# Local attention and whitening on one core: when a new image's terms are moved, four wider shuffles, copied weights straight from DRAM, and VectorE's share of the last image

## The chip, the cores and the metric

The kernel runs on one core of one Trainium2 chip. The metric is the device time of one execution in microseconds (us). The engines named below are TensorE (PE in the profile, with PEld for its weight loads), VectorE (DVE), ScalarE (ACT), GpSimd (POOL) and SyncE (SP). In this kernel SP and POOL mostly issue DMAs, each in its own queue and in order.

## The reference, cut to what matters

```python
# layer 0: a 7x7 convolution with dilation 2 (256 -> 128), a 1x1 one (128 -> 49),
# a softmax over the 49 taps, and a sum of 49 shifted inputs with those weights
k = lax.conv_general_dilated(x, w1, (1, 1), [(6, 6), (6, 6)], rhs_dilation=(2, 2), dimension_numbers=DN) + b1[None, :, None, None]
k = lax.conv_general_dilated(k, w2, (1, 1), [(0, 0), (0, 0)], dimension_numbers=DN) + b2[None, :, None, None]
attn = jax.nn.softmax(k, axis=1)
xp = jnp.pad(x, ((0, 0), (0, 0), (6, 6), (6, 6)))
shifts = jnp.stack([xp[:, :, 2*u:2*u + H, 2*v:2*v + W] for u in range(7) for v in range(7)], axis=1)
x = jnp.einsum('bkchw,bkhw->bchw', shifts, attn)
# layer 1: iterative whitening of each of 4 groups of 64 channels over all pixels
Sigma = EPS * I + jnp.einsum('gdm,gem->gde', xc, xc) / m      # xc: x less its mean
# five Newton steps give wm, the inverse root of Sigma
X_hat = jnp.einsum('gde,gem->gdm', wm, xc)
```

x is (4, 256, 64, 64) in f32: four images of 256 channels.

## The kernel before, in words

Both convolutions are folded into one with 49 output channels, and that one is computed by a two-dimensional fast convolution: rows and columns of the input are combined at seven evaluation points each (`EVAL`), TensorE multiplies point by point, and VectorE interpolates the results back. For an image b the row points are visited in the order `ROWS`, and for each row point the column points come in three banks, `BANKS`: (1, 2, 0), (3, 4, 6) and (5). `conv_step(k, i)` does bank i of row point k on TensorE (`conv_bank`, matmuls on L593) and then lets `prepare` get the same bank of the next row point ready: weights (`weights`, L405), row combination (`row_eval`), column combination (`col_eval`).

**Weights.** The combined weights of a row point and bank are made once, when they are first used, and written to DRAM (`gd`, store on L475); later images load them (L419). For the row points 0, 4 and 5 the row-combined weights themselves lie in DRAM (`kept`). In `weights`, f is the SBUF place that they are loaded to (load on L428): `lgx` for row point 5, the first row buffer `rb[0]` for 4 and 0. VectorE makes the combinations from f into the bank's tile wt (tag wr0, wr1 or wr2, one buffer each), and ScalarE copies those column points that need no combination (`same`, L451, L452 and L461). The first uses of 4 and 5 fall in image 1's convolution, that of 0 in image 2's first steps, which are prepared at the end of image 1's.

**Attention.** The logits of an image are transposed on TensorE into PSUM (L984, a ring of three buffers tagged tp that the other transposes share) and go through `softmax(b, pc)`, once for each parity pc of the columns: VectorE takes maxima (L990), ScalarE does 16 exponentials of 128x49 with a running sum (L998), VectorE scales (L1002 to L1011) and shifts the taps sideways by six in-place shuffles (L1017). The sums are done in quarters of an image, n = 0 to 15 (n // 4 is the image, n % 2 the parity). `move_terms(n)` copies the taps into a padded tile zt by eleven copies (L1058 on ScalarE; for the last image five of the eleven go to VectorE, L1070) and writes it to DRAM in eight DMAs of POOL's queue (L1075); `load_band(n, half)` reads it back skewed, on SP's queue (L1110, L1121). `first_half(n)` and `second_half(n)` then do the sums: `make_block` transposes pieces of the input (L1151) and copies them out of PSUM (xb, L1157, and for the middle pieces xbz, L1165), `weighted_sum` multiplies block by band (L1191), `store_y` writes the result back, `turn_y` transposes it (L1222) and copies it (yt, L1230), and `moments` adds up the Gram matrix (L1243).

**Order.** The halves and softmaxes are planned into eight gaps of each image's convolution (`plan`, `gap`); TensorE's order is the program's (`pe`). On the other engines the tile framework orders instructions by when they are ready in its model and by priority; `tc.high_priority()` raises it, and a manual dependency without a semaphore keeps an instruction behind another on one engine. What the planning does with the last half but one of an image's sums matters here: gap (b + 1, 0) holds `first_half(4b - 1)` and then `soft(b, 0)`, gap (b + 1, 1) holds `second_half(4b - 1)` and then `soft(b, 1)`, and gap (b + 1, 2) holds `first_half(4b)`, for b = 1 and 2. For b = 3 there is no convolution left around them: `second_half(10)` and `soft(3, 0)`, `first_half(11)` and `soft(3, 1)`, `second_half(11)`, `first_half(12)` and so on run one after the other. Before these, `tail` is set, and from there VectorE takes the xb copies and half of `store_y`. In `soft`, the call `bands(4 * b)` moves the new image's first terms at once.

After the sums come the Newton steps (L1441 and around) and the application of the matrices with the output (L1573, L1589).

Of the kernel before, what the change touches and what calls it, by code (L numbers as in the profile page):

```python
# [23 lines left out]
INF = 6  # L24
# [8 lines left out]
def kernel(  # L33
# [371 lines left out]
    def weights(b, br, i, mid=None):  # L405

        first = (br, i) not in made
        made.add((br, i))
        s0 = slot_of[BANKS[i][0]]
        ns = sum(len(taps(bc)) for bc in BANKS[i])
        nk = NSK * len(taps(br)) // 2
        wt = apool.tile([P, ns, NSK], F32, tag=f"wr{i}", name=f"wr_{b}_{br}_{i}")[:, :, :nk]
        w = {bc: wt[:, slot_of[bc] - s0 : slot_of[bc] - s0 + len(taps(bc))] for bc in BANKS[i]}
        if not first:
            nc.sync.dma_start(wt, gd[br][:, s0 : s0 + ns])  # L419
            return w  # L420

        if br in kept:


            f = lgx if br == 5 else rb[0].rearrange("p q r c w -> p (q r c w)")
            f = f[:, : KS * nk]
            if i == 0:
                nc.sync.dma_start(f, kept[br])  # L428
            f = f.rearrange("p (v a r k) -> p v a r k", v=KS, a=NCC, k=KT)
            g = [f[:, v] for v in range(KS)]  # L430
        else:
            g = [gbr[:, v] for v in range(KS)]
        g = [t.rearrange("p a r k -> p (a r k)") for t in g]

        e = ct.rearrange("p a b -> p (a b)") if b else store[4].rearrange("p c r w -> p (c r w)")
        e, o, e1 = (e[:, k * nk : (k + 1) * nk] for k in range(3))
        g0 = [g[KS - 1 - a] for a in range(4)]
        g1 = [g[KS - 5 - a] for a in range(3)]
        o0 = {bc: w[bc][:, 0] for bc in w}
        o1 = {bc: w[bc][:, 1] for bc in w if bc != INF}  # L440

        same = nc.scalar.copy
        if i == 0:
            add(e, g0[0], g0[2])
            add(o, g0[1], g0[3])
            add(e1, g1[0], g1[2])
            add(o0[1], e, o)
            sub(o0[2], e, o)
            add(o1[1], e1, g1[1])
            sub(o1[2], e1, g1[1])  # L450
            same(o0[0], g0[0])  # L451
            same(o1[0], g1[0])  # L452
        elif i == 1:
            madd(e, g0[2], 4.0, g0[0])
            madd(o, g0[3], 4.0, g0[1])
            madd(e1, g1[2], 4.0, g1[0])
            madd(o0[3], o, 2.0, e)
            madd(o0[4], o, -2.0, e)
            madd(o1[3], g1[1], 2.0, e1)
            madd(o1[4], g1[1], -2.0, e1)  # L460
            same(o0[INF], g0[3])  # L461
        else:
            madd(o0[5], g0[0], 2.0, g0[1])
            madd(o1[5], g1[0], 4.0, g1[2])
            madd(o0[5], o0[5], 2.0, g0[2])
            if mid is not None:
                mid()
            madd(o1[5], g1[1], 2.0, o1[5])
            madd(o0[5], o0[5], 2.0, g0[3])
            add(o1[5], o1[5], o1[5])  # L470
        for bc in BANKS[i]:
            f = SCALE[bc] * (SCALE[br] if br not in kept else 1.0)
            if f != 1.0:
                nc.scalar.mul(w[bc], w[bc], f)
        nc.sync.dma_start(gd[br][:, s0 : s0 + ns], wt)  # L475
        return w
# [497 lines left out]
    def softmax(b, pc):  # L974

        lv = logits[b].rearrange("p r w -> p (r w)")
        nm = f"{b}_{pc}"
        mx = work.tile([P, NCH, 2], F32, tag="mx", name=f"mx_{nm}")
        lt = []
        for hf in range(2):  # L980
            lt.append(tp().rearrange("p (i h k) -> p i h k", i=NI, h=2))
            for i in range(NI):
                pe(
                    nc.tensor.transpose(  # L984
                        lt[hf][:, i].rearrange("p h k -> p (h k)")[:, :K2],
                        lv[:K2, bass.ds(2 * (NI * hf + i) * P + pc, P, 2)],
                        ident[:K2, :K2],
                    )
                )
            nc.vector.tensor_reduce(  # L990
                mx[:, NI * hf : NI * (hf + 1)], lt[hf][:, :, :, :KT], AX.X, ALU.max
            )
        nc.vector.tensor_scalar(mx, mx, -1.0, None, ALU.mult)  # L993
        d = terms[b, pc] = bpool.tile([P, 2, NCH, KT], F32, tag="d", name=f"d_{nm}", bufs=2)
        s = work.tile([P, 2, NCH], F32, tag="s", name=f"s_{nm}")
        for h in range(2):
            for i in range(NCH):
                nc.scalar.activation(  # L998
                    d[:, h, i], lt[i // NI][:, i % NI, h, :KT], AF.Exp,
                    bias=mx[:, i, h : h + 1], accum_out=s[:, h, i : i + 1],  # L1000
                )
            nc.vector.reciprocal(s[:, h], s[:, h])  # L1002
            rm = work.tile([P, NCH, KS], F32, tag="rm", name=f"rm_{nm}_{h}")
            nc.vector.tensor_tensor(
                rm,
                s[:, h].unsqueeze(2).to_broadcast([P, NCH, KS]),
                cmask.unsqueeze(1).to_broadcast([P, NCH, KS]),
                ALU.mult,
            )
            dh = d[:, h].rearrange("p i (u v) -> p i u v", u=KS)  # L1010
            nc.vector.tensor_tensor(  # L1011
                dh, dh, rm.unsqueeze(2).to_broadcast([P, NCH, KS, KS]), ALU.mult
            )
        dv = d.rearrange("p h i (u v) -> p (h i u) v", u=KS)
        for v in range(KS):
            if v != R:
                last = nc.vector.stream_shuffle(  # L1017
                    dv[:, :, v], dv[:, :, v], [(c - v + R) % SW for c in range(SW)]
                )

        return last

# [5 lines left out]
    def move_terms(n, after=None):  # L1028
# [9 lines left out]
        for k, (s, j0, nj) in enumerate(MOVES):  # L1038
            u = (s + R) % CR
            m, g = divmod(j0 + u - R, CR)  # L1040
            ne = 2 if u + CR < KS else 1
            i = d[j0 * SW : (j0 + nj) * SW, :, u : u + CR * (ne - 1) + 1 : CR]
            i = bass.AP(
                tensor=i.tensor,
                offset=i[:, :, :, KS - 1].offset,
                ap=[*(list(a) for a in i.ap[:-1]), [-1, KS]],
            )
            o = zt[g * SW : (g + nj) * SW]
            e = R + KS * m + KS - 1 - u
            o = bass.AP(  # L1050
                tensor=o.tensor,
                offset=o[:, e].offset,
                ap=[list(o.ap[0]), [KS * WS, NCH], [(KS - CR) * WS, ne], [1, KS]],
            )

            with tc.high_priority() if n % 4 == 0 else nullcontext():
                if k % 2 == 0 or b < B - 1:
                    ins = nc.scalar.copy(o, i)  # L1058
                    if after is not None:

                        tc.add_manual_dep(
                            ins.ins,
                            after.ins.name,
                            mybir.DependencyInfo(
                                mybir.DependencyClass.NoSync, mybir.DependencyReason.DATA
                            ),
                            reason="move_terms",
                        )
                else:
                    nc.vector.tensor_copy(o, i)  # L1070
# [73 lines left out]
    def make_block(n, m):  # L1144
# [14 lines left out]
        if t8 in (1, 2):  # L1159
            z = ("z", 2 - t8)  # L1160
            if h == 0:
                blocks[n, z] = bpool.tile([P, C], F32, tag=f"xbz{t8}", name=f"xbz_{n}_{t8}")
            i = slice(0, 64) if t8 == 2 else slice(64, P)
            with tc.high_priority():
                nc.scalar.copy(blocks[n, z][h * 64 : (h + 1) * 64], t[i, :C])  # L1165


    PIECES = (
# [48 lines left out]
    def turn_y(n, i):  # L1217
# [9 lines left out]
            )  # L1227
        yb = ybs[n, i] = yt_buf[i % NY]
        with tc.high_priority():
            nc.scalar.copy(  # L1230
                yb.rearrange("p a g c -> p (a g) c")[:, :, :GW],
                t[:, :C].rearrange("p (e c) -> p e c", c=GW),
            )
# [76 lines left out]
    def bands(n, after=None):  # L1310

        move_terms(n, after)
        if n - 1 in half_done:
            load_band(n, 0)
        if n - 1 in done:
            load_band(n, 1)
            move_terms(n + 1, after)

    def second_half(n):
        turn_y(n, 0)  # L1320
        turn_y(n, 1)
        weighted_sum(n, 1, 0)
        weighted_sum(n, 1, 1)
        turn_y(n, 2)
# [20 lines left out]
    def soft(b, pc):  # L1345
        with tc.high_priority() if pc == 0 else nullcontext():
            last = softmax(b, pc)
        soft_done.add((b, pc))
        if pc == 0:
            bands(4 * b)  # L1350

    for b in range(B):
        hs = [
# [279 lines left out]
```

## Time and profile before

| | us |
|---|---|
| median of 3 runs | 741.79 (741.7 to 742.51) |
| the profiled execution | 740.84 |
| its span in the trace | 739.1 |
| TensorE busy in the span | 689.6 (93%) |
| VectorE busy | 581.2 (79%) |
| ScalarE busy | 355.8 (48%) |
| GpSimd busy | 133.4 (18%) |
| mean granted TensorE clock | 0.975 |

The stages as the timeline shows them, with the busy time of each engine:

| stretch (us) | what runs | PE | DVE | ACT | clock |
|---|---|---|---|---|---|
| 0 to 150 | folding of the weights, image 0's convolution | 142.4 | 127.9 | 39.5 | 1.00 |
| 150 to 306 | image 1's convolution, image 0's sums | 148.9 | 132.6 | 85.0 | 0.99 |
| 306 to 452 | image 2's, image 1's sums | 140.6 | 129.4 | 81.3 | 0.99 |
| 452 to 571 | image 3's, image 2's sums | 111.6 | 104.1 | 63.9 | 0.97 |
| 580 to 618 | last softmaxes, n = 10 to 12 | 27.8 | 23.2 | 21.9 | 0.91 |
| 618 to 669 | the other sums of image 3 | 49.9 | 17.0 | 24.2 | 1.00 |
| 669 to 683 | Newton steps | 10.1 | 8.7 | 3.5 | 0.72 |
| 683 to 739.1 | application, output | 49.9 | 32.6 | 31.0 | 0.93 |

A wait in such a profile is read from the idle time of an engine just before an instruction, with the engine and line that released it. A busy share near 100% says that the engine was the bound of that stretch only where the others waited for it.

### The profile page before, as it was taken

What the parts mean: (1) busy time and instruction counts of PE and PEld (TensorE: products, weight loads), DVE (VectorE), ACT (ScalarE), POOL (GpSimd) and SP (SyncE); (2) the same over time, 40 slices, a digit from 0 to 9 for tenths busy, and PEclk for the clock granted to TensorE, in tenths of its full rate; (3) what the DMA queues carried; (4) which work ended last, traced back from release to release, by engine and by line L of the source; (5) the groups of instructions that cost most, each with busy time, mean ns of one, the idle gap of its engine ahead of it and who ended that gap; (6) DMA issues with size and microseconds to landing.
All of it is one profiled execution on the core that took longest, in us unless ns stands there. A gap on an engine that the chain in (4) does not pass through costs nothing. (4 is left out here: it accounts for less than half of the span.)

```text
span 739.1 us, 19180 instructions
## 1 busy us (share of the span) xinstructions
PE 689.6 (93%) x7728; PEld 543.4 (74%) x7728; DVE 581.2 (79%) x1260; ACT 355.8 (48%) x1043; POOL 133.4 (18%) x194
## 2 busy tenths in 40 slices
PE   6999999999998989989999999799999878997996
PEld 1449543478997988878999989798998767895231
DVE  3799998994895899989985999799959564335575
ACT  1424320133755655756554446626546655542564
POOL 0002526664030110020221100202202023300000
PEclk9999999999999999999999999899999999997899
DMA  8923999974673671258746721353623144573587
GB/s 321 256 91 109 243 373 224 229 169 100 165 181 113 243 226 62 67 158 262 188 111 218 245 67 34 73 163 77 186 76 77 45 92 102 119 250 149 228 361 322
DMA packets 77041, 125.20 MB, mean 169 GB/s; under 512 B 36327, under 2 KB 57368, under 8 KB 75800
## 3 DMA queue, kind: packets, MB, share of 16 engines
q1 hardware_dynamic: 64664, 81.88, 34.6%
q0 software_dynamic: 12288, 42.08, 21.9%
q8 instruction: 61, 1.00, 0.6%
q14 instruction: 28, 0.23, 0.1%
HBM read 77.87 MB, written 52.36 MB: 176 GB/s over the span
## 5 line engine op out<-in xcount | busy, mean ns | idle before, releaser
L593 PE MATMUL cv<-xh,wr 128*49 128x128 f32 x4160 | 232.7, 274 | 0.0
L593 PEld LDWEIGHTS cv<-xh,wr 128*49 128x49 f32 x4160 | 227.7, 125 | 3.2 <-issue 1.3
L1075 POOL DMA_DIRECT2D sd<-zt x128 | 67.5, 533 | 324.1 <-ACT zt L1058 290.2
L1191 PE MATMUL y<-band,xb 128*128 128x209 f32 x512 | 115.2, 353 | 3.3 <-DMA band<-sd 2.7
L1191 PEld LDWEIGHTS y<-band,xb 128*128 128x128 f32 x512 | 89.5, 198 | 5.1 <-DMA band<-sd 3.2
L604 ACT COPY pv<-cv 113x486 f32<-113x486 f32 (+2 forms) x60 | 26.0, 433 | 96.2 <-PE cv L593 95.9
L1222 PE MATMUL tp<-ident,slot 128*128 128x128 f32 x256 | 52.9, 304 | 17.9 <-ACT yt L1230 11.0
L1222 PEld LDWEIGHTS tp<-ident,slot 128*128 128x128 f32 x256 | 41.0, 205 | 26.7 <-ACT yt L1230 12.8
L1230 ACT COPY yt<-tp 128x256 f32<-128x256 f32 x128 | 45.3, 376 | 31.5 <-PE tp L1222 30.0
L1058 ACT COPY zt<-d 32x112 f32<-32x112 f32 (+2 forms) x156 | 45.1, 289 | 21.7 <-DVE d L1017 12.5
L354 DVE SCALAR_TENSOR_TENSOR pv<-pv 113x162 f32<-113x162 f32 x176 | 53.3, 322 | 2.1 <-ACT pv L604 1.5
L1151 PE MATMUL tp<-ident,slot 128*128 128x128 f32 x256 | 50.0, 299 | 0.7 <-ACT xbz L1165 0.5
L1211 ACT ACTIVATE slot<-y,pivot 128x512 f32<-128x512 f32 x53 | 36.7, 739 | 24.2 <-PE y L1191 24.2
L998 ACT ACTIVATE d<-tp,mx 128x49 f32<-128x49 f32 x128 | 36.9, 333 | 19.2 <-DVE mx L993 19.1
L1151 PEld LDWEIGHTS tp<-ident,slot 128*128 128x128 f32 x256 | 40.7, 204 | 4.1 <-ACT xbz L1165 0.7
L147 POOL DMA_DIRECT2D slot<-in_x_dram x20 | 33.9, 1696 | 50.2 <-issue 46.0
L354 DVE SCALAR_TENSOR_TENSOR xh<-ct 128x512 f32<-128x512 f32 x40 | 27.1, 700 | 18.5 <-PE cv L593 18.4
L1243 PE MATMUL sig<-yt 128*64 128x65 f32 x1024 | 38.1, 227 | 2.1 <-ACT yt L1230 2.1
L1243 PEld LDWEIGHTS sig<-yt 128*64 128x64 f32 x1024 | 33.3, 140 | 8.3 <-issue 4.3
L758 PE MATMUL acc<-slot,tap 128*49 128x256 f32 (+7 forms) x224 | 34.7, 468 | 0.0
L1157 ACT COPY xb<-tp 128x256 f32<-128x256 f32 x88 | 30.7, 376 | 6.2 <-PE tp L1151 5.8
L1209 DVE TENSOR_SCALAR slot<-y,pivot 128x512 f32<-128x512 f32 x11 | 8.4, 766 | 29.7 <-ACT slot L1211 29.6
(240 smaller groups left out, 1117.5 us busy)
## 6 DMA issues: line engine op xcount, KB each, us to landing
out_dram<-out SPq DMA_DIRECT2D x32, 512.0 KB, 3.6
band<-sd SPq DMA_DIRECT2D x64, 242.0 KB, 3.4
slot<-in_x_dram POOLq DMA_DIRECT2D x20, 512.0 KB, 7.1
sd<-zt POOLq DMA_DIRECT2D x128, 77.0 KB, 2.8
wr<-gd SPq DMA_DIRECT2D x14, 588.0 KB, 4.2
wr<-gd SPq DMA_DIRECT2D x14, 490.0 KB, 3.9
ahead<-in_x_dram POOLq DMA_DIRECT2D x12, 512.0 KB, 7.7
spill<-slot POOLq DMA_DIRECT2D x3, 2048.0 KB, 7.3
```

Source lines behind the costliest of these rows:

```text
L354: return in_turn(STT(o, a, f, b, ALU.mult, ALU.add))
L593: nc.tensor.matmul(o, wv[:, sc, sr, cc], xv[bc][:, h * NCC + cc], start=(j == 0), stop=(j == len(terms) - 1), skip_group_check=True,)
L758: nc.tensor.matmul(ps[h * HB : h * HB + KT, :, o0:o1], w[v][:, cc], rhs, start=(j == 0 and k == 0), stop=(j == len(order) - 1), skip_group ...
L998: nc.scalar.activation(d[:, h, i], lt[i // NI][:, i % NI, h, :KT], AF.Exp, bias=mx[:, i, h : h + 1], accum_out=s[:, h, i : i + 1],)
L1058: ins = nc.scalar.copy(o, i)
L1075: nc.gpsimd.dma_start(bass.AP(tensor=D.tensor, offset=D.offset + h * HS + g * RS, ap=[[LS, TC], [CR * RS, NCH], [1, KS * WS]],), zt[p0 : p ...
L1151: nc.tensor.transpose(t[:, cc * P : (cc + 1) * P], tile_of(xt, cc, t8, h, pc), ident)
L1191: nc.tensor.matmul(ps[:, cc, q0 : q0 + nq, c0:c1], xb[:, cc * P : (cc + 1) * P], rhs, start=(k == 0), stop=(k == len(PIECES[half]) - 1), s ...
L1211: last = nc.scalar.activation(o, i, AF.Identity, bias=pivot[:, cc : cc + 1])
L1222: nc.tensor.transpose(t[:, cc * P : (cc + 1) * P], tile_of(yt, cc, i // 2, i % 2, pc), ident,)
L1230: nc.scalar.copy(yb.rearrange("p a g c -> p (a g) c")[:, :, :GW], t[:, :C].rearrange("p (e c) -> p e c", c=GW),)
L1243: nc.tensor.matmul(sig[g * GW : (g + 1) * GW, cc], yb[:, cc, g, :GW], yb[:, cc, g], start=(count[0] == 0 and cc == 0), stop=(count[0] == 4 ...
```

## The change

There are five edits.

1. In `weights`, row point 4's kept weights are loaded to `lgx` and row point 5's to `rb[0]` (it was the other way round). For the row points in `kept`, `same` no longer copies from f on ScalarE but loads its slice of the kept weights from DRAM into wt, on SP's queue: three transfers of 128x196 for each of the row points 4, 5 and 0. The row points 1, 2 and 3 keep the copies.
2. In `softmax`, for the last image only, VectorE subtracts the maxima (two operations of 128x392 out of PSUM), ScalarE does two exponentials of 128x392 in place instead of 16 of 128x49 with sums, and VectorE sums by two reductions.
3. The six shuffles of one tap column become four of two columns each, which add up to the same shifts: by 1 for columns 4 and 6, by 2 for 5 and 6, and the same to the other side.
4. `soft` calls `bands` for image 0 alone. For the others `second_half(n)` with n % 4 == 3 calls `bands(n + 1, turned)` behind its second `turn_y`, whose ScalarE copy is handed over as the instruction to stay behind; for the last image `move_terms` in `first_half(11)` comes first. The copies of `move_terms` have high priority for n = 0 alone (before: for every first quarter of an image), and for the last image VectorE does all eleven.
5. In the tail, the xbz copies of `make_block` go to VectorE.

```diff
-            f = lgx if br == 5 else rb[0].rearrange("p q r c w -> p (q r c w)")
+            f = lgx if br == 4 else rb[0].rearrange("p q r c w -> p (q r c w)")
...
-        same = nc.scalar.copy
+        def same(o, a):
+            if br in kept:
+                v = KS - 1 - a
+                nc.sync.dma_start(o, kept[br][:, v * nk : (v + 1) * nk])
+            else:
+                nc.scalar.copy(o, g[KS - 1 - a])
...
-            same(o0[0], g0[0])
-            same(o1[0], g1[0])
+            same(o0[0], 0)
+            same(o1[0], 4)
...
-            same(o0[INF], g0[3])
+            same(o0[INF], 3)
...
+        if b == B - 1:
+            for hf in range(2):
+                half = slice(NI * hf, NI * (hf + 1))
+                nc.vector.tensor_tensor(
+                    d.rearrange("p h i k -> p i h k")[:, half],
+                    lt[hf][:, :, :, :KT],
+                    mx[:, half].unsqueeze(3).to_broadcast([P, NI, 2, KT]),
+                    ALU.add,
+                )
+            for h in range(2):
+                nc.scalar.activation(d[:, h], d[:, h], AF.Exp)
+                nc.vector.tensor_reduce(s[:, h], d[:, h], AX.X, ALU.add)
         for h in range(2):
-            for i in range(NCH):
+            for i in range(NCH) if b < B - 1 else ():
...
-        for v in range(KS):
-            if v != R:
-                last = nc.vector.stream_shuffle(
-                    dv[:, :, v], dv[:, :, v], [(c - v + R) % SW for c in range(SW)]
-                )
+        for step, vs in ((1, slice(4, 7, 2)), (2, slice(5, 7)), (-1, slice(0, 3, 2)), (-2, slice(0, 2))):
+            last = nc.vector.stream_shuffle(
+                dv[:, :, vs], dv[:, :, vs], [(c - step) % SW for c in range(SW)]
+            )
...
-            with tc.high_priority() if n % 4 == 0 else nullcontext():
-                if k % 2 == 0 or b < B - 1:
+            with tc.high_priority() if n == 0 else nullcontext():
+                if b < B - 1:
...
-                nc.scalar.copy(blocks[n, z][h * 64 : (h + 1) * 64], t[i, :C])
+                (nc.vector.tensor_copy if tail else nc.scalar.copy)(
+                    blocks[n, z][h * 64 : (h + 1) * 64], t[i, :C]
+                )
...
-            nc.scalar.copy(
+            return nc.scalar.copy(
...
-        turn_y(n, 1)
+        turned = turn_y(n, 1)
+        if n % 4 == 3:
+            bands(n + 1, turned)
...
-        if pc == 0:
-            bands(4 * b)
+        if pc == 0 and b == 0:
+            bands(0)
```

## The prediction

> **What bounds the kernel now.** I read the stage table first: TensorE is busy for 93% of the span, and from 40 to 571 us it stands idle for only about 20 us (read from the same view in windows of 20 us). So a gain must come out of those idle pieces, or out of the 38 us from 580 to 618, where it is busy for 27.8. Next the waits of TensorE over the whole span (us in total, times, longest):
>
> ```profile
> PE tp L1222 <- ACT yt L1230: 11.0, 8, 4.3
> PE y L1191 <- ACT xbz L1165: 5.7, 13, 1.5
> PE tp L1222 <- ACT xbz L1165: 5.6, 3, 3.2
> PE y L1191 <- DMA band<-sd: 2.7, 4, 1.1
> ```
>
> ScalarE, busy for 48%, is the engine waited for: not its load but its order must be at fault. So I went to the timeline at the longest of these waits (start, length, instruction; in brackets the idle time before it and what ended that).
>
> ```profile
> 226.43 0.36 ACT L451 COPY wr<-rb 128x196 f32<-128x196 f32 x1 [3.51 <-DMA rb<-g4d]
> 227.34 0.37 ACT L1165 COPY xbz<-tp 64x256 f32<-64x256 f32 x1
> 227.76 0.63 PE L1222 MATMUL tp<-ident,slot 128*128 128x128 f32 x2 [3.20 <-ACT xbz L1165]
> ...
> 320.88 1.16 ACT L1058 COPY zt<-d 128x56 f32<-128x56 f32 x4 [2.49 <-issue]
> 322.49 0.45 PE L1243 MATMUL sig<-yt 128*64 128x65 f32 x8 [0.93 <-ACT yt L1230]
> ...
> 465.53 2.39 ACT L1058 COPY zt<-d 128x56 f32<-128x56 f32 x8 [4.52 <-issue]
> 468.27 0.66 ACT L1230 COPY yt<-tp 128x256 f32<-128x256 f32 x2
> 468.70 0.70 PE L1222 MATMUL tp<-ident,slot 128*128 128x128 f32 x2 [4.30 <-ACT yt L1230]
> ```
>
> Three times ScalarE stands at the head of its queue before a copy whose data is late, with ready copies behind it that TensorE needs: a weight copy waiting for row point 4's load, then a new image's terms (images 1 and 2) waiting for VectorE's shuffles (these end at 320.4 and 465.1). Each wait costs more than its length. In the windows (length, busy times, granted clock ahead of the last two figures):
>
> ```profile
> 228.00:230.00 2.00, 2.00 (x8) 1.81 (x8) 1.93 (x4) 1.95 (x7) 0.00 (x0) 0.50 0.00 0
> 328.00:330.00 2.00, 2.00 (x22) 2.00 (x20) 1.63 (x4) 0.68 (x4) 1.01 (x2) 0.50 0.92 247
> 470.00:472.00 2.00, 2.00 (x7) 1.57 (x5) 1.44 (x5) 1.26 (x4) 1.86 (x4) 0.50 0.36 48
> ```
>
> After each wait TensorE runs at half clock: about 3.3 us after the first, 3.2 after the second, 4.6 after the third. Half of that is lost: 1.65, 1.6 and 2.3 us.
>
> Last, the tail, by the starts of the moments that close each half (TensorE's timeline), with the one VectorE line that ends the worst of them:
>
> ```profile
> 578.55 1.15 PE L1243 MATMUL sig<-yt 128*64 128x65 f32 x32
> 590.96 1.15 PE L1243 MATMUL sig<-yt 128*64 128x65 f32 x32
> 602.53 1.15 PE L1243 MATMUL sig<-yt 128*64 128x65 f32 x32
> 609.98 2.29 DVE L1070 COPY zt<-d 64x112 f32<-64x112 f32 x10
> 617.34 1.15 PE L1243 MATMUL sig<-yt 128*64 128x65 f32 x32
> 623.62 1.15 PE L1243 MATMUL sig<-yt 128*64 128x65 f32 x32
> 631.30 1.15 PE L1243 MATMUL sig<-yt 128*64 128x65 f32 x32
> ```
>
> The last two intervals are undisturbed: 6.3 us for a second half, 7.7 for a first. The three before took 12.4, 11.6 and 14.8; less 7.7, 6.3 and 7.7, and less 1.2 each for the softmax transposes in the first two, 14.8 us are lost there. Two of the three tp buffers hold the logits until the last of 16 exponentials (582 to 589, then 597 to 605, about 0.28 us from one to the next), and ScalarE waits 3.8 and 3.7 us for the shuffles before it copies terms.
>
> **The change, part by part.**
>
> *Weights (A).* Row point 4's load no longer waits for `rb[0]` (SP stood there from 217 to 220.8, then 4.5 us to land); row point 5's load into `lgx` went out at 179, long before its use, and this one can do the same. ScalarE's copy is gone too. TensorE's wait of 3.2 us and the 1.65 of half clock go: at most 4.9. VectorE doesn't hold this back: it waits 6.6 us for TensorE just after, until 238.56. I take -4.5. The nine copies become nine transfers on SP. Each waits until TensorE has left the bank's wt, as VectorE's writes into wt do already, and the next use comes two banks later, over 10 us; landing takes 2.8 us (the 77 KB transfers) to 4.2 (the 588 KB ones), so they cost 0. The store on L475 now waits for them, and the bands behind it on SP with it: without cover, about 3 us for each of three row points, +9. Row point 5's `rb[0]` is free from 220.8; row point 0 reloads it only after 262.7 instead of 244, and VectorE reads that at 283.
>
> *Terms of images 1 and 2 (B, C).* The copies now stay behind `turned`. At 465 that decides: the first two yt copies and the eviction on L604 were queued behind eight term copies and now go at about 462.5. TensorE could gain 4.3 + 2.3 = 6.6. But VectorE is idle for only 5.3 of the 20 us from 460 to 480 and then busy for 39.97 of 40, so less is kept: bounds 0 (terms still ahead of the later yt copies) and -5.3; I take C = -4. At 320 the first two yt copies were ahead already. There the third and fourth wait for term copies, which only start 0.6 us earlier by the shorter shuffles, unless priority puts yt ahead. Waits 3.1 (0.93, 1.19 and 0.94) and clock 1.6 could go, 4.7 in all; VectorE is idle for 3.9 us from 320 to 360: bounds 0 and -3.9; B = -1, near the low end, since the order may stay. The eight POOL transfers and the band loads that follow move with the copies. Behind them on SP stand weight loads (L419), which waited 180 us in all for TensorE; the new image's first band is needed at 341 and came 1.1 us late already.
>
> *Shuffles (E).* Six took 3.3 us, 0.54 from one start to the next. No row has a width of 224. Bounds: no dearer, 4 x 0.54 = 2.2 us (-1.1 per softmax), and in proportion to width, 4 x 1.08 = 4.3 (+1.0). Between 56 and 392 columns VectorE's products go from 212 to 563 ns, 1.04 ns a column; so 0.66 each, 2.6 in all, -0.6. Six softmaxes lie in convolutions, where VectorE is full in parts: of -3.6 I take -0.5 on the path.
>
> *Last image (D).* ScalarE loses 32 exponentials (9 us) for 4 of 0.53, and 24 term copies of 0.29. VectorE gains per softmax two subtractions (0.56 by the products) and two reductions (0.556) less 0.6 of shuffles: 1.6, and 24 term copies of 0.21. Logits leave tp after the subtractions, at about 583 rather than 589. From 581 VectorE has per softmax maxima 1.2, subtractions 1.1, sums 1.1, scaling 2.0, shuffles 2.6: 8 us; with the xb, xbz and store copies of n = 11 in between (some 4 us) the shuffles end at 591 to 593, not 595.2. Terms 2.3, POOL's eight issues 4.3, landing 2.8 and the band 3.4 follow; by the same steps the first sum of n = 12 starts at 602.5 to 605 instead of 606.2. There TensorE waits some 3 us, as it arrives earlier, and loses perhaps 1.5 to the clock. After that it no longer meets the block of 609.98 (terms of n = 13 ahead of the xb copies; waits of 2.4 and 0.5, half clock 1.6), as the second softmax is through by about 603. -2.7 - 4.5 + 1.5 is -5.7; bounds -14.8 and, if VectorE is the bound, +16.7 (below); D = -5.
>
> *xbz on VectorE in the steady tail.* Now 0.44 and 0.37 in two engines with 0.06 of handover, once per n on the chain; two xb copies on VectorE in a row take 0.76: -0.1 for three n, F = -0.3.
>
> Sum: -4.5 - 1 - 4 - 0.5 - 5 - 0.3 = -15.3. The profiled execution would go from 740.84 to 725.5 (1.7 of it outside the span); it lies 0.95 under the median, so the median goes from 741.79 to **726.5**.
>
> On the clock, the Trainium skill ("TensorE: Matmul & The Clock Gate", Part 1: The HAM clock gate) says that half clock comes after one idle window of some 3.4 us. The trace disagrees in part: near 325 no wait was over 1.2 us, and half clock came. By the page nothing of B's 1.6 would be due to the waits, and D's new wait of 3 us would lose nothing (-6.5 rather than -5).
>
> **Rivals.**
>
> - *Only the weights' wait goes.* The shuffles still hold ScalarE up, as each yt copy may stand behind terms: B = C = 0. For it: order is by a model, and terms stood ahead of yt at 320. Against: `turned` at 462. 741.79 - 4.5 - 0.5 - 5 - 0.3 = 731.5. Chance 0.20.
> - *Nearly all goes.* A 4.9, B 3, C 5.3, D 11, E 1.5, F 0.3: 26, so 716. Against: VectorE's full stretches and the band's chain. 0.10.
> - *The bands come late.* Terms moved later push the first band of images 1 and 2 behind a weight load on SP (the next went out at 342.3, 5.7 us after the band): two waits of about 6 with clock, +12. 741.79 - 15.3 + 12 = 738.5. For it: the 1.1 us at 343. 0.08.
> - *VectorE becomes the bound of the tail.* Added to its queue between 580 and 665: 2 x 1.6 of softmax, 24 terms at 0.21 = 5.0, and 20 xbz at 0.42 = 8.4; 16.7 in all, in front of xb copies that TensorE waits for. If all of it is on the path: 741.79 - 10.3 + 16.7 = 748. It turns the result slower once over 10.3 of the 16.7 lie there. Against: VectorE is idle for 15 of the 38 us and 34 of the next 51. 0.08.
> - *Nothing comes through*: VectorE, full from 255 to 322 and from 480 to 520, takes back A to C, and the band keeps the tail. 741.8. 0.04.
>
> **How the numbers follow.** The forecast has 0.50 and reaches from 719 to 733. The range 715 to 739 adds the first rival, most of the second and half of the third: about 0.8. This kernel's runs can tell 0.2% (1.5 us) from no change: faster 0.88, same 0.04, slower 0.08.
>
> **What would show it.** A: no wait of ScalarE for g4d, and full clock at 228. B, C: no wait of over 2 us for yt in images 2 and 3. D: the moments at 590.96 and 602.53 come 9 us or less after the ones before, the ones at 617.34 about 6 us earlier counted from 578.55, and VectorE over 75% busy there. E: shuffles 0.6 to 0.7 us apart. I am wrong if TensorE shows new waits for VectorE's xb or xbz over 5 us in the tail, or for bands over 3 us after 340.

## The result, and the profile after

| | before | after |
|---|---|---|
| median (us), 9 runs each, side by side | 742.39 | 738.01 (735.02 to 741.18) |
| ratio, 95% interval | | 0.9934 [0.9909, 0.9959] |
| profiled execution / its span | 740.84 / 739.1 | 736.93 / 735.2 |
| PE, DVE, ACT busy | 689.6, 581.2, 355.8 | 687.0, 594.5, 332.6 |

By the ratio the change gains 4.9 us [3.0, 6.8] (4.4 by the medians) where 15.3 were forecast. Of two kernels below, the bands alone on GpSimd's queue and the copies alone back on ScalarE, the profiled execution was a slow one (1368.7 and 1009.6 us), so it is left out of their times and its trace is not read. The waits that the forecast started from are gone, and others stand in their place. The view of TensorE's waits over the span (us in total, times, longest), after:

```profile
PE y L1210 <- DMA band<-sd: 10.1, 4, 5.2
PE y L1210 <- ACT xbz L1182: 5.7, 10, 1.5
PE tp L990 <- ACT xb L1174: 3.5, 2, 1.9
PE tp L1241 <- ACT yt L1249: 3.0, 6, 0.8
```

The wait for yt fell from 11.0 to 3.0 and the one of L1222 for xbz (5.6 before) is no longer among the first; the wait for bands rose from 2.7 to 10.1.

Where it went is read from a ledger: the start of each `moments` call on TensorE, after less before. What happens between two of them changes the difference by just that much. Each kernel has one trace, so differences of a few tenths in it are not told from chance.

| moments at (before) | 212.8 | 232.2 | 320.9 | 347.7 | 472.1 | 506.4 | 578.6 | 591.0 | 602.5 | 617.3 | 665.8 |
|---|---|---|---|---|---|---|---|---|---|---|---|
| after less before | +1.53 | -1.00 | -0.84 | +0.13 | -6.00 | -2.60 | -2.57 | -5.03 | -8.73 | -3.88 | -3.54 |

The +1.53 ahead of 212.8 is a band that came 1.80 us late at 194 (0.18 before); in the kernels below the same spot stands between -0.37 and +1.53 with no order that follows the edits, so it is put to none. The weights give 2.53 up to 232; image 1's terms take 0.97 by 347.7; image 2's give 6.13 by 472.1 and 3.40 of it comes back by 506.4; the last image gives 6.16 by 602.5 and 4.85 comes back by 617.3; the steady tail takes 0.34.

The timeline of after at these places, in order of time (start, length, instruction; in brackets the idle time before it and what ended that):

```profile
227.34 0.53 ACT L480 ACTIVATE wr<-wr 128x392 f32<-128x392 f32 x1 [1.12 <-DVE wr L347]
228.58 0.51 PE L1168 MATMUL tp<-ident,slot 128*128 128x128 f32 x2 [1.08 <-ACT xbz L1182]
230.58 0.69 PE L1210 MATMUL y<-bandz,xbz 128*128 128x96 f32 x4 [0.78 <-ACT xbz L1182]
...
339.12 0.33 SPq L419 DMA_DIRECT2D wr<-gd  x1
339.63 0.66 SPq L1127 DMA_DIRECT2D band<-sd  x1
343.57 0.98 PE L1210 MATMUL y<-band,xb 128*128 128x209 f32 x4 [2.50 <-DMA band<-sd]
...
467.96 1.56 ACT L1075 COPY zt<-d 32x112 f32<-32x112 f32 x5
469.55 1.32 ACT L1230 ACTIVATE slot<-y,pivot 128x512 f32<-128x512 f32 x2
471.17 0.73 PE L990 MATMUL tp<-ident,lgx 113*128 113x113 f32 x4 [1.59 <-ACT xb L1174]
...
602.93 1.76 PE L1210 MATMUL y<-band,xb 128*128 128x209 f32 x4 [5.15 <-DMA band<-sd]
603.09 5.31 DVE L1087 COPY zt<-d 128x56 f32<-128x56 f32 x22
608.43 0.42 DVE L1174 COPY xb<-tp 128x256 f32<-128x256 f32 x1
609.37 0.70 PE L1168 MATMUL tp<-ident,slot 128*128 128x128 f32 x2 [0.56 <-DVE xbz L1182]
```

The same two DMAs and the same sum of before, at the second place:

```profile
338.70 0.36 SPq L1110 DMA_DIRECT2D band<-sd  x1
342.29 0.54 SPq L419 DMA_DIRECT2D wr<-gd  x1
343.44 0.98 PE L1191 MATMUL y<-band,xb 128*128 128x209 f32 x4 [1.13 <-DMA band<-sd]
```

Four places. At 227 ScalarE no longer waits for a weight copy, but it stands before the next instruction of the same list, the scaling of the weights, until VectorE has made them. In both kernels image 1's first band leaves SP only when a weight load ahead of it has its place free, at 335.24 (336.62 before). New in after is the next weight load: it goes at 339.12, ahead of the band that the second sum needs, where before all four bands went first. That band leaves 0.93 us later and lands at 343.53, hardly later than before (343.40); but TensorE was ready for it at 341.07 rather than 342.31, so its wait is 2.50 us instead of 1.13. At 468 the term copies are still ahead of the store and of xb. And in the last image the first band is 5.15 us late, and then 22 term copies in a row (two quarters' worth) hold VectorE for 5.31 us with the xb copies behind them.

The clock follows. The view of windows of after (length; busy PE, PEld, DVE, ACT, POOL; then granted clock, DMA share, GB/s):

```profile
598.00:600.00 2.00, 0.00 (x0) 0.00 (x0) 1.96 (x10) 0.24 (x1) 0.82 (x2) 0.60 0.83 154
602.00:604.00 2.00, 1.07 (x3) 1.04 (x4) 1.86 (x8) 0.00 (x0) 0.00 (x0) 0.50 0.82 201
610.00:612.00 2.00, 2.00 (x8) 1.84 (x7) 1.05 (x4) 0.00 (x0) 2.00 (x5) 0.50 0.72 138
612.00:614.00 2.00, 1.90 (x26) 1.47 (x27) 1.30 (x4) 0.43 (x1) 1.87 (x4) 0.98 0.88 210
```

Half clock from 598.42 to 612.07, while ScalarE is nearly idle and VectorE nearly full.

### The profile page after: what moved, and what is told of

It is laid out like the page before. It is cut to its first block, busy times and chain, and to the rows that moved or that the text cites. A ratio compares the mean times of both kernels' runs of the same rounds, so it can differ in the third digit from the quotient of the medians.

```text
span 735.2 us, 19094 instructions
## 1 busy us (share of the span) xinstructions
PE 687.0 (93%) x7728; PEld 541.8 (74%) x7728; DVE 594.5 (81%) x1280; ACT 332.6 (45%) x930; POOL 133.2 (18%) x194
## 4 chain that ended last, share of the span: by engine, by line
PE 37%; DVE 26%; issue 9%; ACT 9%; POOL 4%; DMA 4%; SPq 0%; POOLq 0%; ACTq 0%; DVEq 0%
PE cv L599 16%; PE y L1210 6%; PE tp L1594 4%; DVE xh L354 3%; PE sig L1262 3%; DVE pv L354 3%; POOL ahead L147 3%; PE tp L1241 3%; DVE zz L354 2%; DMA band<-sd 2%; PE tp L1168 2%; DVE rb L347 2%; DVE rb L354 1%; ACT zt L1075 1%; POOL sd L1092 1%
## 5 line engine op out<-in xcount | busy, mean ns | idle before, releaser
L1210 PE MATMUL y<-band,xb 128*128 128x209 f32 x512 | 113.0, 347 | 10.3 <-DMA band<-sd 10.1
L1210 PEld LDWEIGHTS y<-band,xb 128*128 128x128 f32 x512 | 87.5, 195 | 12.1 <-DMA band<-sd 9.1
L1075 ACT COPY zt<-d 32x112 f32<-32x112 f32 (+2 forms) x132 | 38.2, 290 | 10.6 <-DVE d L1034 4.7
L1016 ACT ACTIVATE d<-tp,mx 128x49 f32<-128x49 f32 x96 | 27.5, 332 | 19.2 <-DVE mx L999 19.2
```

What stands on the lines that cost most here:

```text
L1210: nc.tensor.matmul(ps[:, cc, q0 : q0 + nq, c0:c1], xb[:, cc * P : (cc + 1) * P], rhs, start=(k == 0), stop=(k == len(PIECES[half]) - 1), s ...
```

## The experiments

Each is timed beside the kernel before; ledger figures are against before. The theories carry letters in the expectations.

**Which edit does what.** Three kernels, each the kernel before with a part of the change: edit 1 alone (the weights), edit 4 without its VectorE copies (terms moved later), and edits 2 and 5 with the VectorE term copies (the last image).

> The kernel before with edit 1 alone (row point 4 to lgx, 5 to rb[0], copies of kept weights from DRAM). Theory L (the ledger of the two traces): the wait of 3.20 us of TensorE at 227.8 and the half clock behind it go, but two waits of about 1 us for xbz take their place and the first band near 194 comes 1.5 us later, so the moments that closed at 249.86 come about 1 to 2.5 us earlier and the whole is -1 us or less. Theory F (the forecast's sizes): -4.5 us, and the first band near 194 is not touched (a wait of 0.2 us as before).

> The kernel before with edit 4 alone, less the last image's copies on VectorE: terms of images 1, 2 and 3 moved a half later and at normal priority. Theory L: the wait of 4.30 us at 468.7 goes, and the moments there come 6 us earlier, but 3 to 3.5 us of it are given back by 505; around 325 the waits stay, and the first band of image 2 comes late by over 2 us; -2 us in images 1 and 2, and in the tail up to +3 for image 3's terms. Theory F: -5 us before the tail.

> The kernel before with the last image's softmax, all its term copies and the tail's xbz on VectorE, but the terms moved at once and at high priority and the six shuffles as before. Theory K (the chain from the softmax over terms, POOL and SP to the band sets the first sum of n = 12, wherever the move stands in the order): TensorE still waits 4 us or more for the band before that sum and runs at half clock behind it; -1 to -2 us. Theory M (moving the terms a half later made the band late): the wait is under 2 us, and -5 us.

| | ratio | us saved |
|---|---|---|
| weights alone | 0.9959 [0.9941, 0.9978] | 3.0 |
| terms later alone | 1.0006 [0.9991, 1.0021] | none that shows |
| last image alone | 0.9979 [0.9969, 0.9990] | 1.6 |

The weights alone show the same two waits (1.08 and 0.79) as after. The terms alone trade the wait of 4.30 us for a band 3.90 us late at 346.5 and short waits around 473 to 476. The last image alone has the late band of after almost to the hundredth. Its timeline:

```profile
605.81 1.76 PE L1205 MATMUL y<-band,xb 128*128 128x209 f32 x4 [5.17 <-DMA band<-sd]
```

So that wait comes neither from the moved terms nor from the shuffles, but from the last image's own edits. The weights and the last image come to 4.6 of the 4.9 us.

**Shuffles left out.** After without any shuffle, so that the taps are not shifted sideways:

```diff
-        for step, vs in (...): last = nc.vector.stream_shuffle(...)
+        last = None
```

> The kernel after without any shuffle: the taps are not shifted sideways, so the output is another one. VectorE has 2.9 us less to do per softmax, 23 in all. If VectorE is the bound from 468 to 505 of what was gained there (37.7 us between the moments at 466.1 and 503.8), that stretch shrinks by 2 us or more and the whole by over 6 us; if it is TensorE's own work or a transfer, the stretch stays within 1 us and only the tail's first band comes earlier, by about 3 us.

724.18 us (2 runs), ratio 0.9753 [0.9732, 0.9775]. The stretch between the moments of 472.1 and 506.4 is 32.91 us (after 37.66, before 34.26), with one wait of 0.96 and no half clock. But the term copies also come 1.8 us sooner behind the turned copies ahead of them, so this doesn't tell VectorE's load from ScalarE's order.

**Bands of images 1 and 2 on GpSimd's queue**, away from the weight loads:

```diff
+        queue = nc.gpsimd if n in (4, 8) else nc.sync
...
-            nc.sync.dma_start(band ...
+            queue.dma_start(band ...
```

> The kernel after, with the band loads of the first quarter of images 1 and 2 (n = 4 and 8) in POOL's queue instead of SP's. Theory Q (the first band is ready by about 330 but stands behind three weight loads on SP, which wait for TensorE until 335): the band leaves by 331, the wait of 2.50 us at 343.6 goes, the moments that started at 347.8 come about 2.5 us earlier, and the whole is -2.5 us against the kernel after. Rival (the transfers themselves are slow): the wait stays over 1.5 us.

734.63 us (3 runs), ratio 0.9884 [0.9867, 0.9900]: 3.4 under after (medians of different sessions, here and below).

**The same, with the terms kept behind the store** (the `bands` call behind the second turn removed, so that the terms wait for `store_y`):

> As the run before it, and the terms of images 1 and 2 stay behind the store that closes the second half instead of behind its second transposed piece. Theory O (what was gained at 466 was given back because the term copies now stand between the later yt copies, the store and the xb copies on ScalarE): the waits of 0.96 and 1.90 us at 322 to 325 and of 0.95 and 1.59 at 468 to 471 go, with the half clock behind the latter, so the stretch from the moments at 466 to the next ones shrinks by about 4 us, and the whole is -5 to -8 us against the run before it, as long as the bands still come in time. Theory V (the forecast's: VectorE is full from 480 to 520 and takes the gain back): the stretch shrinks by less than 1 us.

735.04 us, ratio 0.9882 [0.9860, 0.9903]. The waits at 322 to 325 and 468 to 471 and their half clock are gone, but two come: 4.41 us for the band at 338.9, and 2.91 us for yt at 495.85. The second, in its timeline:

```profile
494.54 0.66 ACT L541 COPY xh<-rb 128x512 f32<-128x512 f32 x1 [6.96 <-DVE rb L354]
495.85 0.70 PE L1242 MATMUL tp<-ident,slot 128*128 128x128 f32 x2 [2.91 <-ACT yt L1250]
```

ScalarE stands before a copy whose input VectorE hasn't made, with yt behind it: VectorE is late, though it has had no idle piece of over 0.1 us since 473.1. The stretch from 472.1 to 506.4 takes 36.06 us.

**Half of the last image's term writes on SP's queue**, to halve GpSimd's 4.3 us of issuing:

```diff
-                nc.gpsimd.dma_start(
+                (nc.sync if n >= 12 and h else nc.gpsimd).dma_start(
```

> The kernel after, with half of the eight transfers that write the last image's terms to DRAM in SP's queue, which is idle then. Theory K (the chain from softmax over copies, eight issues of 0.53 us on POOL and the band loads is the bound of the tail): the wait of 5.15 us for n = 12's band falls to about 3, and the whole is -2 to -3 us against the kernel after. Rival: the landing, not the issue, is what counts, and nothing changes.

742.98 us, ratio 0.9994 [0.9973, 1.0015]: 5 us worse than after. A miss: the first of n = 13's writes stood on SP from 596.7 to 605.9, 9.3 us, waiting for VectorE's terms, in front of n = 12's bands, and TensorE waited 11.12 us. So it doesn't tell what halving the issues is worth.

**Term copies and xbz of the last image back as before** (half of the terms on ScalarE, xbz on ScalarE; the softmax of edit 2 stays):

> The kernel after, with the tail's xbz copies and six of the last image's eleven term copies back on ScalarE (edit 5 and half of the copies undone); the softmax stays on VectorE. Theory K with VectorE's load in the chain: four xbz (1.7 us) and half of the copies (1.2 us) come out of it, the wait for n = 12's band falls from 5.15 to about 2.5 us, -3 us. Rival: ScalarE again stands before term copies that wait for shuffles, yt copies behind it, and TensorE waits over 1.5 us for yt; no change or slower.

732.82 us (3 runs), ratio 0.9863 [0.9839, 0.9887]: 5.2 under after (the next expectation takes 4.3, the median of all four executions). Two things go back at once, the terms and xbz, and no run parts them. The next runs hold this edit and the bands on GpSimd's queue.

**Both repairs together, and two more edits on top**: terms behind the store, and n = 12's writes alone split between SP and GpSimd.

> The changed kernel with two edits: the bands of the first half image of images 1 and 2 are loaded from GpSimd's queue, so that they no longer stand behind the nine weight loads on SyncE's queue (the run with that edit alone came out about 3.3 us below the change), and the last image's copies of the terms and of the turned boundary channels are put back as they were in the kernel before (that edit alone: about 4.3 us below the change). Theory S, the two places are apart (320 to 345 and 590 to 680 us) and their gains add: 738.0 - 3.3 - 4.3 = 730.4 us; in the trace the first sum after 340 waits less than 0.5 us for its band, and the first sum of the last image starts about 2.5 us earlier after the moments at 578.55 (before's count) than the 24.4 us of the change, with a wait of under 3 us for its band instead of 5.15. Theory R, the last image is bound by the transfers between its sums and not by VectorE: the gain of the second edit was in the disturbed spread of few runs, the wait stays at 5 us, and the time is that of the bands' edit alone, 734.7 us.

> As the run before (bands of images 1 and 2 from GpSimd, copies of the last image as before), and the term copies wait for the store of the first half image (the order that the kernel before had in the compiler's list), without the earlier dependency on the copy of the turned sums. Theory V, VectorE fills the 36 us after 472 whatever the order: the waits for the turned sums and the turned input at 468 to 472 go, but 2.9 us come back at 495 as in the earlier run of this order, and the time is that of the run without it, within 1 us. Theory O, the order of ScalarE's copies is what gave the gain at 472 back: the stretch from the moments at 472 to those at 506 falls from 37.7 us to under 35, and the time is 2 us lower than without it.

> As the run with bands of images 1 and 2 from GpSimd and the copies of the last image as before, and half of the writes of the first terms of the last image (n = 12 alone) are issued by SyncE, the other half by GpSimd. The earlier run that did this for all four half images lost 5 us because the second's writes stood on SyncE ahead of the first's bands; here they do not. Theory Q, GpSimd's issuing of eight writes in 4.3 us is a link of the chain from the shuffles' end to the first sum: the first band lands about 2 us earlier, the wait of TensorE shrinks by 2 us, and the time falls by about 2 us. Theory T, the transfers themselves (the writes' landing and the band's landing) are the chain and the issues lie beside them: under 0.7 us.

| | us | ratio |
|---|---|---|
| both repairs | 729.97 | 0.9837 [0.9817, 0.9858] |
| and terms behind the store | 728.75 | 0.9817 [0.9796, 0.9837] |
| and n = 12's writes split | 728.01 | 0.9801 [0.9781, 0.9820] |

The repairs add up (730.4 expected). With both, the first band of image 1 leaves at 328.84 (336.62 before), the band wait after 340 is gone and the moments of 347.7 come 2.74 us earlier than before instead of 0.13 later. In the last image the ledger goes from -5.46 at 578.6 to -12.09 at 617.3: 6.63 gained where after has 1.31. Timeline and windows of that kernel at the place shown above:

```profile
589.54 4.29 POOL L1092 DMA_DIRECT2D sd<-zt  x8 [18.11 <-ACT zt L1075]
598.44 1.76 PE L1209 MATMUL y<-band,xb 128*128 128x209 f32 x4 [3.96 <-DMA band<-sd]
598.59 1.79 ACT L1075 COPY zt<-d 128x56 f32<-128x56 f32 x6 [3.65 <-DVE d L1034]
598.60 2.30 DVE L1087 COPY zt<-d 64x112 f32<-64x112 f32 x10
600.93 0.42 DVE L1175 COPY xb<-tp 128x256 f32<-128x256 f32 x1
```

```profile
598.00:600.00 2.00, 1.56 (x5) 1.41 (x6) 1.78 (x7) 1.36 (x5) 0.00 (x0) 0.51 0.90 244
600.00:602.00 2.00, 2.00 (x10) 1.84 (x9) 1.28 (x5) 1.09 (x4) 1.55 (x3) 0.64 0.90 187
602.00:604.00 2.00, 2.00 (x16) 2.00 (x15) 1.09 (x3) 1.10 (x3) 2.00 (x5) 1.00 0.63 123
```

The band is still late, by 3.96 us and not under 3 as expected. But the copies share two engines, xb goes at 600.93 with TensorE never waiting again for long, and full clock is back by 602 instead of 612. From the first sum to the next moments it takes 6.81 us (598.44 to 605.25); after took 10.53 (602.93 to 613.46).

The split of the writes is inconclusive: the intervals overlap, and in its trace the first sum comes 25.23 us after the moments of 578.6, against 25.35. It doesn't tell GpSimd's issues from the transfers either: with the split two bands leave SP at 596.04 and 596.60 (595.75 and 596.91 without), and the first sum starts only when the second of them has landed (599.35), so a change of their order may hide what the split gained. The terms behind the store: 1.2 us, inside the intervals too; the ledger gains 0.44 at the end, the stretch takes 36.56 us instead of 37.69, and 2.80 us of wait for yt come at 494, as in the earlier run of that order.

**What was left of the terms and of the weights.** Three more on top of both repairs: the terms allowed only behind the fourth turn, the scaling moved off ScalarE, and both.

```diff
+                if i == 0 and br in kept:
+                    nc.vector.tensor_scalar(w[bc], w[bc], f, None, ALU.mult)
+                else:
                     nc.scalar.mul(w[bc], w[bc], f)
```

> Reference for this run is the version with the bands of images 1 and 2 on GpSimd's queue and the last image's copies as before (729.97 us), which has the change's order of the terms: allowed after the second turn of the sums, so that 11 of ScalarE's copies stand between the third turn's copy, the fourth's and the store, with waits of TensorE of 0.95 us for the turned sums and 1.58 us for the turned input around 465 to 468 and half clock behind them. Here the terms are allowed only after the fourth turn's copy: ahead of the store, but behind all turned sums. Theory O, ScalarE's order gave the gain back: the wait for the turned sums goes; if the store and the turned input still stand behind the terms a wait of about 3 to 4 us for the turned input stays, else the time falls by 1 to 2 us; the stretch from the moments at 472 to those at 506 (37.69 us) falls to 36 or below only if both waits go. Theory V, VectorE is full from 472 to 506 whatever ScalarE does: whatever is gained at 465 to 472 comes back as a wait near 495 for turned sums behind a copy that waits for VectorE, and the time stays within 1 us.

> Reference is again the version of 729.97 us. The scaling of the first group's weights of the filters kept in DRAM (two instructions of 128x392) moves from ScalarE to VectorE, so that ScalarE no longer waits for VectorE's last product with the copies of the turned input behind it. Theory W, that wait is the rest of the weights' gain: the waits of 1.08 and 0.78 us for the boundary channels near 228 to 231 us go, the moments after them start about 1.9 us earlier than in the changed kernel, and the time falls by 1.5 to 2 us. Theory X, VectorE is full there (its list from 220 to 230 us has no gap), so that two more instructions delay the input's sums and TensorE's next batch by 0.6 us or more, and the time falls by less than 0.7 us or not at all.

> Both edits of the two runs before together. They lie 240 us apart, so the gains should add: 729.97 us plus the two differences, within 1 us.

| | us | ratio |
|---|---|---|
| terms behind the fourth turn | 731.19 | 0.9853 [0.9836, 0.9871] |
| scaling on VectorE | 727.30 (726.3 to 728.6) | 0.9799 [0.9782, 0.9815] |
| both | 728.84 | 0.9817 [0.9802, 0.9831] |

The terms behind the fourth turn gain nothing: the wait for yt at 465 goes, xb still waits 1.17, and 2.15 us come at 497; image 1's bands are late again by 1.48 and 1.68. Both together give 728.84 where adding gives 728.5. The scaling on VectorE settles the weights. Its timeline:

```profile
226.06 0.66 DVE L481 TENSOR_SCALAR wr<-wr 128x392 f32<-128x392 f32 x2
227.22 0.69 PE L1212 MATMUL y<-bandz,xbz 128*128 128x96 f32 x4 [0.20 <-ACT xbz L1186]
227.83 1.15 PE L1264 MATMUL sig<-yt 128*64 128x65 f32 x32
```

The two instructions cost VectorE 0.66 us, and both waits near 228 are gone: the ledger stands at -4.36 at 232 and -4.12 at 320.9. At the last moments this kernel's ledger stands at -14.34. That is close to the -15.3 that the forecast summed, but with three more edits, so it doesn't bear the forecast out. Its median is 10.7 us under after, the lowest of the kernels that compute the whole result; the interval overlaps that of the split.

## Why the prediction was right and wrong

The measured 738.01 lies outside the forecast's 719 to 733 and beside the 738.5 of the rival with the late bands. That is a coincidence: the two waits of about 6 us that the rival adds did not come, and the missing gain went in every part.

**Weights (A): the mechanism held, the size didn't.** Forecast -4.5, measured -2.53 between the moments of 212.8 and 232.2. The step that failed is "TensorE's wait of 3.2 us and the 1.65 of half clock go". ScalarE's queue has the scaling right behind the copy, and what the copy no longer waits for, the scaling does: 1.08 + 0.78 = 1.86 us. With the scaling elsewhere the term reads -4.48 (+0.12 to -4.36). The nine transfers cost nothing that shows.

**Image 1's terms (B): wrong in sign.** Forecast -1, measured +0.97. The step that failed is that "The eight POOL transfers and the band loads that follow move with the copies" was told and given no price. With the terms later, a weight load of 339.12 stood ahead of the second sum's band on SP. The band landed no earlier than before, the wait for it grew from 1.13 to 2.50 us, and all that had been gained by then was lost. The parts show that it is the move of the terms: in the weights alone that load goes at 340.48, behind all the bands, and the wait is 1.28; in the terms alone it goes at 340.70, ahead of a band of 341.90, and the wait is 3.90. With the bands on another queue the term reads -1.69 (-1.05 to -2.74), and -1.18 in the last kernel but one; there the bands are free of the earlier weight loads as well, so part of this was to be had without moving the terms. The rival of the late bands named the mechanism, at two waits of 6; it was one of 2.5, for image 1 alone. That the second image escaped is seen (no band wait from 455 to 512) and was not tried.

**Image 2's terms (C): in size nearly right.** Forecast -4, measured -6.13 and then +3.40, so -2.73. The forecast's reason, that VectorE is full and less is kept, holds in this form: the orders that shorten the waits at 465 to 472 (behind the fourth turn, behind the store) get 2.2 to 2.9 us of wait back at 494 to 497, behind ScalarE's copy on L541 that stands waiting for VectorE, and the stretch still takes 36.0 to 36.8 us against 37.7 with the change's order and 34.26 before. So 0.9 to 1.7 of the 3.40 is ScalarE's order with the half clock that it brings. The other 1.7 stays in every order. That it is VectorE's load is likely by that copy, with VectorE never idle for over 0.1 us in the 21 us before it, and by the 32.91 without shuffles, but no run took load from VectorE without moving the terms as well, so it is not shown.

**Last image (D): the largest miss.** Forecast -5, measured -1.31, and the sign of being wrong came: a band 5.15 us late (3 was the bound). The first half of the step is right: the shuffles end at 592.0 (591 to 593 forecast), the first sum starts at 602.93 (602.5 to 605), and both halves before it are faster by 6.16. The step that failed is "After that it no longer meets the block of 609.98 ... as the second softmax is through by about 603". The softmax ends at 603.0, and the block comes with it: 22 term copies on VectorE ahead of xb, 5.31 us at a time when ScalarE is idle. With it the clock was mis-sized: the wait was 5.15 us rather than 3, and half clock lasted to 612.07 rather than costing 1.5. In after the block itself is followed by a wait of only 0.56, at half clock; in two other kernels with the same block the wait for xbz behind it is 1.49 (terms behind the store) and 1.89 (last image alone). The rival "VectorE becomes the bound of the tail" had this mechanism, but counted as a load spread over 85 us; it decided in one place. Putting the copies back gives -6.63, so the softmax edit, with the shuffles and without the copies, does all that D was forecast to do and more. This is no single trace's doing: the term reads -5.7 to -6.9 in the six kernels with the copies back and -0.95 to -2.3 in after, the last image alone and the terms behind the store. Which of the two copies put back, terms or xbz, is worth how much is not shown.

**Shuffles (E)** start 0.62, 0.81 and 0.73 us apart (0.66 forecast, 0.6 to 0.7 the sign), with 27.4 us busy before and 24.7 after over eight softmaxes, 0.34 saved on each (0.6 forecast). **xbz (F)**: forecast -0.3, measured +0.34; with xbz back on ScalarE the steady tail reads -0.09.

By the signs that the prediction set: full clock at 228 and no wait for g4d came true, as did no wait over 2 us for yt and VectorE at 89% (33.67 of the 38 us from 576), and the moments at 591 and 602.5 within 10.0 and 7.9 us of the ones before (9 was the bound; the first missed it). The moments of 617.3 came 1.3 us earlier counted from 578.6, not 6.

On the clock, after the waits of 0.96 and 1.90 us near 322 half clock came again (325.35 to 328.77) without any single long window, against the one-window rule that the prediction weighed. The prediction's 4.6 us of half clock after the third wait of before is a little short: it ran to 473.74, 5.0 us.

## What to carry to other kernels

When a wait at the head of an in-order queue is taken away, read the next few entries of that queue: the next one with a late input inherits the stall. A DMA that moves later in program order can end up behind a transfer that used to stand behind it, one that waits for the engine that needs the DMA, so it needs a price or another queue. And a load that is small over a whole stage decides in the one place where it stands in a block ahead of what the bounding engine needs: here it paid to split the term copies between two engines that finished together.

## What the hardware showed

The clock changes in steps. In every trace here half clock lasts 3.41 us or a whole multiple of it, save for the last piece that the end cuts off, and so does full clock between two pieces of half clock. So what a wait costs depends on where it falls: 2.15 us at 497.19 (terms behind the fourth turn) were followed by one step of half clock, 2.17 us at 494.92 (that and the scaling on VectorE) by none. Counted in steps from the clock's changes, the first wait lies in one step, and an end of a step at 493.7 cuts the second.

In after the band's wait ended at 602.93, but waits of 0.64 and 0.56 us followed, at 606.18 and 609.37, and full clock came only at 612.07, after four steps. With both repairs no wait of over 0.2 us followed the one that ended at 598.44, and full clock was back at 601.43, after one step. Half of the time at half clock being lost, the waits of 5.15 and 3.96 us cost about 4.5 us of clock in the one and 1.5 in the other. That the short waits held half clock up is likely and not shown: before the output of the kernel with the terms behind the store TensorE has no wait from 675.9 on, and half clock still lasts to 682.98, two steps.

A shuffle's start-to-start time went from 0.54 us at 112 columns to about 0.7 at twice the columns, so most of it is not per column. Two scalings of 128x392 in a row take 0.95 us on ScalarE (at 231.54 before) and 0.66 on VectorE.
